# Spacing out the row scatters of a routed group in a fused attention and mixture-of-experts kernel

## The chip, the cores and the metric

The kernel runs on one core of one Trainium2 chip. The metric is the device time of one execution in microseconds (us). The kernel before the change takes 2172.19 us, the median of three runs between 2167.95 and 2175.05 us.

## What is computed

The input is 8 sequences of 1024 tokens, each token 256 float32 numbers. The reference first does `x = x + layernorm(attention(layernorm(x)))`, with 16 heads of 16 numbers and a causal mask, and then `x = x + layernorm(moe(layernorm(x)))`. The second part is what the change touches. A router gives each token scores for 8 experts; the two best experts are used with the softmax scores as weights:

```
scores = softmax(flat @ router_weight.T + router_bias)
topk_w, topk_idx = top_k(scores, 2)
gate = min(gu[..., :I], 7); up = clip(gu[..., I:], -7, 7)
down = ((up + 1) * gate * sigmoid(1.702 * gate)) @ down_proj + down_bias
out = (down[chosen] * topk_w).sum()
```

The reference computes all 8 experts for every token. The kernel computes only the two chosen ones: it sorts the tokens by expert in DRAM first.

## The kernel before

**Groups and units.** The tokens are 16 groups of 512 (t = 0 to 15), two for each sequence b. Attention runs sequence by sequence in units u of four heads: four units for a sequence, 32 in all. While the scores of unit u are computed once to find the row maxima (`sa`, L834), the scores of unit u-1 are computed again transposed, exponentiated and multiplied with the values (`sb` L929, `pT` L941, `av` L970). A unit is 9 steps of two **half steps** each, so a unit is 18 half steps and a sequence 72. After unit 31 one more round of 9 half steps does the values of the last unit alone.

**What is done in between.** Everything else of the attention part is written as generators that yield pieces: `piece(pe, dve, act, pool, after)` states what the next piece costs each engine, and that it is ready `after` half steps behind the piece before it. After each half step `pump` (L1253) adds a planned allowance to a credit for each engine (for GpSimd 1.91 us a half step, with a ceiling of 1.3) and emits ready pieces as long as every engine that they need has a credit of at least zero. Three lists are gone through in this order: `urgent` (masks, maxima and normalisation of the running units), the first job of `due` (layernorm and projections of the next sequence, which have to be there at given units), and all of `back`. The `back` list holds one job for each group, `finish(b, c)` (L1017), oldest first.

**A `back` job.** It projects the attention result (`yps`, L1031), takes its layernorm, adds x and stores the sum (`x1d`, L1052). Then it waits until the job two groups before it is done (L1053), and goes on to `route(t)` (L1074): the second layernorm (`xn`), its transposes (`x2ps`, L1092), the router logits (`lps`), softmax, ranks, the count of tokens for each expert (`cps`, L1153), the slots in DRAM (L1181), two extra columns of `xn` (L1186 and L1190), and then the eight **scatters** (L1191 to L1200): indirect DMAs issued by GpSimd, each of which writes 128 rows of `xn` to the slots of one of the two choices. The projection of a group (L1022) also waits until the job two groups before it has its `xn`. The job is done when its last scatter is issued. Jobs 11 and 15 go on to `table` (L301), which works out which expert each tile of 256 sorted rows belongs to.

**The hand-over.** When unit 31 has been emitted and the table of the first 12 groups isn't known yet, the oldest `back` jobs are emitted on the spot, with no allowance asked (L1383 to L1385), until it is; then the first sorted rows are loaded (`load_early`). The expert part then runs tile by tile. The first 14 tiles pump the rest of the `back` jobs, 12 times a tile, and before tile 14 `finish_all` (L1270) emits whatever is left.

**Order on the queues.** TensorE, VectorE, ScalarE and the SP queue run in the order of the source. On GpSimd `in_order` keeps the order of the source too, except that neighbouring scatters may change places. GpSimd also runs the causal masks (L950, L883), the reciprocal roots (L517) and most of the layernorm scaling (L529, L1050), and in the expert part one multiplication for each quarter tile (L1477).

Of the kernel before, what the change touches and what calls it, by code (L numbers as in the profile page):

```python
# [24 lines left out]
def piece(pe=0.0, dve=0.0, act=0.0, pool=0.0, after=0):  # L25


    return (pe, dve, act, pool), after
# [30 lines left out]
def attn_moe_kernel(  # L59
# [31 lines left out]
    NT = B * S // TB  # L91
# [147 lines left out]
    def in_order(put, scatter=False):  # L239

        if free[0]:
            return
        for before_it in fixed if scatter else fixed + loose:
            tc.add_manual_dep(
                put.ins, before_it,
                mybir.DependencyInfo(mybir.DependencyClass.NoSync, mybir.DependencyReason.DATA),
                reason="order of the source",
            )
        if scatter:
            loose.append(put.ins.name)  # L250
        else:
            fixed[:], loose[:] = [put.ins.name], []

    def apart(put, group):

        tc.declare_no_dep(put.ins, group=group, reason="scatters to different rows")
        tc.add_to_no_dep_group(group, put.ins)
# [284 lines left out]
    with ExitStack() as attn:  # L542
# [229 lines left out]
        n = QC // P  # L772
# [244 lines left out]
        def finish(b, c):  # L1017
# [35 lines left out]
            while nth > 1 and not finishes[nth - 2].done:  # L1053
                yield piece(after=1)
            yield from route(nth, y, last)

        def normed(dst, src):
# [16 lines left out]
        def route(t, x1, last):  # L1074
# [90 lines left out]
            for n in range(NTB):  # L1165
                nc.vector.tensor_tensor(slot[:, n, :], slot[:, n, :], so_far, ALU.add)
                after = counts[:, nth + 1, :]
                if n + 1 < NTB:
                    after = small.tile([P, E], F32, tag="after", name="after")
# [18 lines left out]
            first_of = ap2.tile([P, NTB, E], F32, tag="rank", name=f"first_{t}")  # L1188
            nc.vector.tensor_tensor(first_of, is_r[:, 0], region, ALU.mult)
            nc.vector.tensor_reduce(xn[:, :, D + 1], first_of, AX.X, ALU.add)  # L1190
            for r in range(TOPK):  # L1191
                for n in range(NTB):
                    yield piece(pool=1.1, after=0 if last and (n or r) else 1)
                    put = nc.gpsimd.indirect_dma_start(  # L1194
                        out=xs_dram[:, :],
                        out_offset=bass.IndirectOffsetOnAxis(ap=slots[:, t, r, n : n + 1], axis=0),
                        in_=xn[:, n, :], in_offset=None,
                    )
                    in_order(put, scatter=True)
                    apart(put, "xs")  # L1200
# [561 lines left out]
```

## Time and profile before

| what | before |
|---|---|
| median of the timed runs | 2172.19 us |
| the profiled execution, and its span | 2175.62 us, 2173.9 us |
| mean granted TensorE clock | 0.981 |
| TensorE busy | 2064.7 us (95%) |
| VectorE busy | 1712.1 us (79%) |
| ScalarE busy | 1061.4 us (49%) |
| GpSimd busy | 1059.4 us (49%) |
| unit 0 starts; unit 31 starts; round 32 starts; first expert tile | 24.3, 1313.1, 1355.4, 1386.8 us |
| scatters (L1194) | 128, median 976 ns each |

A table of where the groups stand was read from the timelines of VectorE and GpSimd. The half steps were counted on VectorE, which takes the maxima of each half step with its own instructions (L844, L850, L859, L865); h is the running number, 18 for each unit. "Ready" is the last column of `xn` (L1190); `x1d` is the store of the group two later, behind which that group's `route` may begin once this group's job is done.

| group | ready, us (h) | first scatter, us | last scatter, us | `x1d` of the group two later, us |
|---|---|---|---|---|
| 2 | 579.0 (249) | 579.4 | 606.5 | 630 |
| 3 | 639.7 (276) | 641.4 | 656.9 | 677 |
| 4 | 762.2 (330) | 764.6 | 780.3 | 801 |
| 5 | 823.7 (355) | 824.2 | 846.7 | 873 |
| 6 | 937.2 (402) | 939.6 | 955.4 | 975 |
| 7 | 997.6 (427) | 998.1 | 1020.2 | 1046 |
| 8 | 1110.8 (474) | 1113.1 | 1128.9 | 1150 |
| 9 | 1172.6 (499) | 1173.1 | 1195.4 | 1217 |
| 10 | 1276.3 (541) | 1276.8 | 1294.2 | 1300 |
| 11 | 1315.5 (558) | 1316.0 | 1332.7 | 1371 |

How to read it: the profile's busy shares are means over a long kernel. Attention (24 to 1387 us) and the expert part have different limits, so times are read from windows that cover one sequence (four units) each, where the work is the same from one to the next.

### The profile page before, as it was taken

What the parts mean: (1) busy time and instruction counts of PE and PEld (TensorE: products, weight loads), DVE (VectorE), ACT (ScalarE), POOL (GpSimd) and SP (SyncE); (2) the same over time, 40 slices, a digit from 0 to 9 for tenths busy, and PEclk for the clock granted to TensorE, in tenths of its full rate; (3) what the DMA queues carried; (4) which work ended last, traced back from release to release, by engine and by line L of the source; (5) the groups of instructions that cost most, each with busy time, mean ns of one, the idle gap of its engine ahead of it and who ended that gap; (6) DMA issues with size and microseconds to landing.
All of it is one profiled execution on the core that took longest, in us unless ns stands there. A gap on an engine that the chain in (4) does not pass through costs nothing.

```text
span 2173.9 us, 44649 instructions
## 1 busy us (share of the span) xinstructions
PE 2064.7 (95%) x16205; PEld 1265.7 (58%) x16205; DVE 1712.1 (79%) x4090; ACT 1061.4 (49%) x2068; POOL 1059.4 (49%) x1217
## 2 busy tenths in 40 slices
PE   7999999999999999999999998999999999999995
PEld 3444444444444434444534443678888888888884
DVE  4786887986887887887878788678767888877776
ACT  3566665666666655655655665433123232222222
POOL 3321653472474456355554645565544444544443
PEclk9899999999999999999999999999999999999998
DMA  4102102112112111112111111646867777766774
GB/s 123 19 17 46 31 29 64 34 45 45 43 35 65 26 38 46 48 46 49 48 36 41 43 38 36 222 161 213 266 247 257 269 264 264 266 240 239 270 269 152
DMA packets 147097, 254.85 MB, mean 117 GB/s; under 512 B 21505, under 2 KB 106009, under 8 KB 144953
## 3 DMA queue, kind: packets, MB, share of 16 engines
q1 hardware_dynamic: 133128, 217.01, 32.2%
q0 software_dynamic: 12528, 34.36, 4.2%
q8 instruction: 129, 2.11, 0.4%
q14 instruction: 96, 0.78, 0.1%
q10 hardware_dynamic: 1216, 0.58, 0.1%
HBM read 171.13 MB, written 55.63 MB: 104 GB/s over the span
## 4 chain that ended last, share of the span: by engine, by line
PE 69%; DVE 18%; POOL 6%; issue 3%; ACT 1%; DMA 1%; DVEq 0%; ACTq 0%; POOLq 0%; SPq 0%
PE sa L834 18%; PE gu L1461 14%; PE av L970 10%; PE dn L1501 7%; PE sb L929 6%; PE pjk L740 3%; PE yps L1031 3%; PE pjq L740 3%; PE vps L726 3%; DVE mx L850 2%; DVE sa L844 2%; DVE acc L1576 1%; POOL ytd L1514 1%; DVE gate L1470 1%; POOL xsd L1194 1%
## 5 line engine op out<-in xcount | busy, mean ns | idle before, releaser
L941 ACT ACTIVATE pT<-sb 128x512 f32<-128x512 f32 x1134 | 616.7, 595 | 394.9 <-PE sb L929 363.5
L929 PE MATMUL sb<-qP,kP 32*128 32x512 f32 (+3 forms) x3072 | 706.1, 528 | 13.4 <-ACT pT L941 11.1
L834 PE MATMUL sa<-kP,qP 32*128 32x512 f32 (+3 forms) x3072 | 656.9, 528 | 24.7 <-DVE mx L844 12.6
L1461 PE MATMUL gu<-xsT,wg 128*128 128x256 f32 (+1 forms) x2208 | 489.4, 374 | 3.1 <-ACT xsT L1441 1.9
L1461 PEld LDWEIGHTS gu<-xsT,wg 128*128 128x128 f32 x2208 | 410.0, 191 | 59.0 <-ACT xsT L1441 3.1
L850 DVE TENSOR_REDUCE mx<-sa 128x2 f32<-128x1024 f32 x256 | 310.7, 1215 | 118.1 <-PE sb L929 90.4
L950 POOL TENSOR_SCALAR_AFFINE_SELECT pT<-pT 128x512 f32<-128x512 f32 x256 | 164.5, 659 | 467.4 <-ACT pT L941 456.1
L834 PEld LDWEIGHTS sa<-kP,qP 32*128 32x128 f32 x3072 | 227.5, 185 | 248.2 <-issue 102.7
L1472 ACT ACTIVATE sig<-gate 128x256 f32<-128x256 f32 (+1 forms) x276 | 112.8, 409 | 530.6 <-DVE gate L1470 498.6
L970 PE MATMUL av<-pT,vpad 128*32 128x256 f32 (+1 forms) x5120 | 350.8, 371 | 5.0 <-DVE avs L981 3.0
L929 PEld LDWEIGHTS sb<-qP,kP 32*128 32x128 f32 x3072 | 295.4, 186 | 46.3 <-ACT pT L941 21.1
L1477 POOL TENSOR_TENSOR sig<-sig,gate 128x256 f32<-128x256 f32 (+1 forms) x276 | 199.5, 725 | 244.1 <-ACT sig L1472 240.9
L970 PEld LDWEIGHTS av<-pT,vpad 128*32 128x32 f32 x5120 | 117.3, 109 | 294.4 <-issue 237.1
L1501 PE MATMUL dn<-wd,act 128*128 128x256 f32 x1064 | 259.6, 383 | 17.5 <-DVE act L1482 15.7
L1501 PEld LDWEIGHTS dn<-wd,act 128*128 128x128 f32 x1064 | 194.2, 190 | 50.8 <-DVE act L1482 26.7
L1470 DVE TENSOR_SCALAR gate<-gu,bs 128x256 f32<-128x256 f32 (+1 forms) x276 | 128.9, 467 | 115.2 <-PE gu L1461 96.5
L844 DVE CUSTOM_DVE_ANT_0 sa<-sa,cmask 128x512 f32<-128x512 f32 x256 | 177.6, 698 | 39.8 <-PE sb L929 20.9
L1514 POOL DMA_INDIRECT ytd<-ys,places x133 | 133.8, 1006 | 128.5 <-DVE ys L1509 93.8
L1194 POOL DMA_INDIRECT xsd<-xn,slots x128 | 128.9, 1007 | 65.0 <-DVE xn L1190 35.5
L1482 DVE SCALAR_TENSOR_TENSOR act<-up,sig 128x256 f32<-128x256 f32 (+1 forms) x276 | 123.3, 447 | 25.8 <-POOL sig L1477 25.6
L869 ACT COPY edge<-sa 128x512 f32<-128x512 f32 x192 | 112.9, 588 | 40.9 <-DVE mx L859 20.1
L888 DVE TENSOR_REDUCE mx<-edge 128x8 f32<-128x1024 f32 x96 | 115.7, 1205 | 18.2 <-POOL edge L883 18.2
(243 smaller groups left out, 2343.8 us busy)
## 6 DMA issues: line engine op xcount, KB each, us to landing
wg<-_L_ffn_gate_up_proj_dram SPq DMA_DIRECT2D x69, 1024.0 KB
wd<-in_L_ffn_down_proj_dram SPq DMA_DIRECT2D x69, 512.0 KB
xs<-xsd SPq DMA_DIRECT2D x60, 258.0 KB
yy<-ytd SPq DMA_DIRECT2D x15, 1024.0 KB
bs<-biasd SPq DMA_DIRECT2D x69, 132.0 KB
x<-in_L_attn_x_dram SPq DMA_DIRECT2D x16, 512.0 KB
aT<-avn SPq DMA_DIRECT2D x256, 32.0 KB
x1d<-y SPq DMA_DIRECT2D x16, 512.0 KB
```

The lines of the kernel that those rows point to most:

```text
L834: nc.tensor.matmul(ps[:, hh, ds(at, w)], lhsT=qP[r, ts(i, P)], rhs=kP[r, ds(c * QC, w)], start=True, stop=True,)
L844: nc.vector.tensor_tensor_reduce(out=ps[:, hh, :], in0=ps[:, hh, :], in1=cmask, scale=1.0, scalar=NEG, op0=ALU.add, op1=ALU.max, accum_out ...
L850: nc.vector.tensor_reduce(mx[:, heads, i, 2:3], ps, AX.X, ALU.max)
L929: nc.tensor.matmul(banks[hh][:, ds(at, QC - off)], lhsT=kP[r, ts(j, P)], rhs=qP[r, ds(c * QC + off, QC - off)], start=True, stop=True,)
L941: nc.scalar.activation(pT[:, 2 * pair + hh, :], banks[hh], AF.Exp)
L950: in_order(nc.gpsimd.affine_select(out=d, in_=d, compare_op=ALU.is_ge, fill=0.0, base=0, pattern=[[0, HG], [1, P]], channel_multiplier=-1,))
L970: nc.tensor.matmul(av[ds(hh * HS, HS), ds(off + a - at, z - a)], lhsT=vp[:, j, ds((g * HG + hh) * VS, HS)], rhs=pT[:, hh, a:z],  start=c n ...
L1194: put = nc.gpsimd.indirect_dma_start(out=xs_dram[:, :], out_offset=bass.IndirectOffsetOnAxis(ap=slots[:, t, r, n : n + 1], axis=0), in_=xn ...
L1461: nc.tensor.matmul(ps[:, half, :w], lhsT=wg[:, kt, ds(half * FF + f * P, P)], rhs=xT[:, kt, :], start=(kt == 0), stop=(kt == KT - 1),)
L1477: in_order(nc.gpsimd.tensor_tensor(sg, sg, gt, ALU.mult))
L1501: nc.tensor.matmul(pss[n][:, 0, :], lhsT=act[:, f, ts(n, P)], rhs=wd[:, f, :], start=(f == 0), stop=(f == FT - 1),)
L1514: put = nc.gpsimd.indirect_dma_start(out=yt_dram[:, :], out_offset=bass.IndirectOffsetOnAxis(ap=places[:, i, n : n + 1], axis=0), in_=y[:, ...
```

## The change

In `route`, the pieces of the eight scatters of a group get other distances. Before, each was ready one half step behind the piece ahead of it (in the two groups of the last sequence, the seven later ones at once). After, the first is ready two half steps behind the slots in all groups, and each later one four half steps behind the one before; in the last two groups they are ready at once, as before. The condition `t == NT - 2` decides nothing, since `last` is true for group 14 as well as 15. No instruction is added or removed.

```diff
+            rest = 0 if last else 1 if t == NT - 2 else 4
             for r in range(TOPK):
                 for n in range(NTB):
-                    yield piece(pool=1.1, after=0 if last and (n or r) else 1)
+                    yield piece(pool=1.1, after=rest if n or r else 2)
                     put = nc.gpsimd.indirect_dma_start(
```

## The prediction

> **What bounds the kernel now.** I first cut attention into windows of one sequence each (four units, 72 half steps), because the work in them repeats. These are the sequences b = 2 to 7.
>
> ```profile
> core 0: us, PE busy (x) PEld busy (x) DVE busy (x) ACT busy (x) POOL busy (x), PEclk, DMA share, GB/s
> 336.30:500.60 164.30, 160.80 (x1538) 75.57 (x1534) 135.54 (x310) 102.36 (x191) 90.94 (x98) 1.00 0.19 47
> 500.60:665.30 164.70, 161.68 (x1578) 76.74 (x1574) 137.49 (x316) 104.70 (x196) 85.02 (x93) 1.00 0.18 44
> 665.30:840.40 175.10, 167.73 (x1582) 78.13 (x1578) 139.59 (x324) 105.24 (x197) 76.56 (x84) 0.97 0.17 43
> 840.40:1014.00 173.60, 166.44 (x1586) 78.51 (x1582) 140.73 (x326) 104.49 (x197) 91.17 (x98) 0.98 0.17 45
> 1014.00:1189.20 175.20, 167.18 (x1582) 78.34 (x1578) 140.88 (x325) 104.51 (x197) 91.45 (x98) 0.97 0.17 44
> 1189.20:1355.40 166.20, 152.03 (x1558) 70.53 (x1555) 140.88 (x331) 99.92 (x189) 91.03 (x102) 0.99 0.15 39
> ```
>
> The second column is the length. TensorE is busy for 98% of the first two windows, so it is the bound; VectorE has 83%. TensorE's instruction counts in the next three windows are the same within 1%, yet they take 10.4, 8.9 and 10.5 us longer than the 164.7 before, 29.8 us in all, and their clock column falls below 1.00. By units, all of it lies in the third and fourth unit of a sequence (47.4 and 44.9 us in the first case, where the sequence before has 41.7 and 40.2). So I opened the timelines of one such place, 998 to 1009 us, on GpSimd, VectorE, ScalarE and TensorE:
>
> ```profile
> 998.06 1.10 POOL L1194 DMA_INDIRECT xsd<-xn,slots  x1 [4.75 <-DVE xn L1190]
> 999.46 0.96 POOL L1194 DMA_INDIRECT xsd<-xn,slots  x1 [0.30 <-issue]
> 1000.73 0.96 POOL L1194 DMA_INDIRECT xsd<-xn,slots  x1 [0.30 <-issue]
> 1001.99 0.96 POOL L1194 DMA_INDIRECT xsd<-xn,slots  x1 [0.30 <-issue]
> ...
> 1004.01 1.23 DVE L850 TENSOR_REDUCE mx<-sa 128x2 f32<-128x1024 f32 x1 [4.04 <-PE sa L834]
> ...
> 1004.12 1.09 ACT L941 ACTIVATE pT<-sb 128x512 f32<-128x512 f32 x2 [5.02 <-PE sa L834]
> ...
> 1004.76 1.61 PE L929 MATMUL sb<-qP,kP 32*128 32x512 f32 x4 [1.77 <-ACT pT L941]
> ...
> 1007.36 1.22 PE L834 MATMUL sa<-kP,qP 32*128 32x512 f32 x2
> ```
>
> While GpSimd issues four scatters back to back, VectorE and ScalarE stand still for 4 to 5 us, both waiting for scores whose matmuls the timeline ends at 1000.0; then TensorE stands for 1.8 us because ScalarE has freed no bank; and a little later `sa` takes 1.22 us where it takes 0.70 at full clock. The trace grants half clock for 3.4 us from 1007.2.
>
> I then went through all 576 half steps for the time by which VectorE's maximum starts later than both its scores and its own last instruction allow. More than 1 us is found eight times: 1.5 and 1.5 (group 0), 1.6 (group 4), 4.4 (5), 1.6 (6), 4.0 (7), 2.3 (8) and 4.3 us (9). Each lies inside a run of four or five scatters 1.27 us apart. Of the groups 1, 2, 3, 10 and 11, which go out in ones, twos and threes but for one run of four (group 2), none shows it. The half clock follows all six of groups 4 to 9, for 6.8, 3.4, 3.4, 3.4, 6.8 and 3.4 us, so half of 27.2 us is lost, 13.6. With the six late starts (18.2 us) that is 31.8 us, close to the 29.8 from the windows. I take 29.8, and 3.0 more for group 0.
>
> A rule speaks against this reading. The Trainium skill, SBUF — State Buffer, section "SBUF: two separate sides", has only VectorE and GpSimd contend, and TensorE and ScalarE wait on no one for their SBUF ports; by it a run of scatters could not hold up scores and exponentials, the stalls would have another cause, and the gain would be nothing. The trace shows the standstill and the scatters together in seven groups of seven, so I go by the rows. TensorE: Matmul & The Clock Gate, section "Why this matters for your kernels", asks for idle gaps over some 3 us before the clock drops; the gaps here are 1.8 to 2.1 us and it drops six times, so the rows decide again (by the rule 18.2 us would be the price, not 31.8).
>
> **The change, part by part.**
>
> *Distance 4.* Number and cost of the 128 scatters stay (976 ns each). A half step is 164.7 / 72 = 2.29 us, so the scatters of a group in attention become ready 9.2 us apart and cannot queue up four at a time unless GpSimd has nothing else for some 12 half steps; the masks come in the first ten half steps of each unit, so three in a row is what can still happen (half steps 11, 15 and 19). Group 3 has such a run at 650 us, without a late maximum. I let a fifth of the 32.8 us stay: gain 26. The ends are 0 and 33.
>
> *First scatter at 2.* GpSimd waits 35.5 us in 8 places for the last column of `xn` with a scatter at the head of its queue. Queued behind it are masks, roots and scaling. TensorE waits only 13.6 us in all for masks (`av` on `pT`), 20 times, so the gain is between 0 and 13.6 and a loss at most one half step per group, which is hidden while the group isn't due. I take 0.
>
> *Lateness, in attention.* The last scatter of a group comes 2 + 28 = 30 half steps behind "ready", where the least before was 8: 22 half steps or 50 us later. Three things wait for it: `route` of the group two later, the table at group 11, and the first loads. Before, `x1d` comes 20 to 26 us behind the last scatter two groups earlier (780.3 to 801, 846.7 to 873 and so on), so the wait now takes hold: group 6 ends at 402 + 30 = 432 and not 410, and group 8 may begin there and not at 417. What it then needs is VectorE time, which is scarce in the first ten half steps of a unit, and TensorE credit, which the next sequence's projections take first. Going through the pieces, group 8 is ready at about 475 (before 474), since it then waits for fewer others. An odd group is hit harder: group 7's last scatter is near 457 to 475, so the second layernorm of group 9 comes after 458, its count of tokens (`cps`) just misses the projections that begin at half step 496, and it is ready near 517 (before 499). That repeats and does not grow. Group 11 then starts `route` at 548, and 25 to 30 half steps later, at 573 to 578, it is ready. Unit 31 ends at 576.
>
> *The hand-over.* So eight scatters and the whole table of group 11 are emitted on the spot. Before, half of the table was already:
>
> ```profile
> 1355.42 0.82 PE L417 MATMUL tabps<-two,ones 128*128 128x144 f32 x2 [3.06 <-DVE two L414]
> 1357.50 0.57 PE L438 MATMUL takenps<-each,ones 128*128 128x8 f32 x2 [1.26 <-DVE each L435]
> ```
>
> These 4.3 us become the whole chain. VectorE's table instructions from L310 to L356 take 2.3 us, and the copy of `seg` with its round trip about 0.7: 3.0 us more, and some 2 us if the slots aren't ready (`cps` to `slots` took 2.9 us for group 12). The eight scatters then are the longest run of all, in front of the masks of round 32: one stall of the above size, 5 us (29.8 / 6). Less what overlaps: 8 us in all. If the group is ready ten half steps sooner it is 3; if its logits aren't done it is 20 or more. On the SP queue the first four sorted loads stand behind the last scatter, and behind them the transfers of the last unit (issued 1366.7 us before) and the first weights (1375.6): the run would end near 1363, so nothing there is late.
>
> *Expert part.* Group 12 now does its whole route here, 7.9 us of planned VectorE cost more (the pieces from L1105 to L1190), at 1.4 a quarter tile (175.1 us from 1386.8 to 1561.9 for 14 tiles are 12.5 us a tile, 3.1 a quarter): 18 us. Much of this is hidden: its gate for group 14 moves from 1403 to about 1445, against `x1d` of 14 at 1443. Distance 4 is 4 pumps of 1.04 us here. Before, the last table pieces come at 1565 us, at the very end of the 14 pumped tiles, so there is no slack: I put 4 us on forced pieces and filled gaps. The ends are -3 (scatters of groups 12 and 13 no longer hold up L1477; 1.2 to 2.0 us gaps on `dn`) and 15.
>
> Sum: -26 + 8 + 4 = -14, to about 2161.5 for the profiled execution of 2175.62; its distance to the median (3.4) goes along: **2158**.
>
> **The rivals.**
>
> 1. *The jobs fall behind more than that.* If job 9 and 11 lose another 20 half steps, group 11 has no logits at unit 31's end, and the chain from layernorm to table is emitted with nothing between: stats, root, four scalings of 1.23 us, transposes, logits, about 20 us, ranks and slots 10, table 7, the run of scatters 5, and as much as 15 at `finish_all`: -26 + 57 = +31; with half of that +10. 2175 to 2203, slower. It decides from about 10 half steps later than I reckon. For: the limits are tight. Against: groups 12 and 13 have no projections beside them. Chance 0.18.
> 2. *The stalls stay*, since not the run of scatters but the transfers that lie beside it make them (at 1000 us SP is sending the queries and keys of the next unit). Then only the cost is left: +5 to +15, 2177 to 2187. For: group 2's run of four, with no other transfers, has no stall. Against: the units with single scatters and the same transfers have none either. Chance 0.14.
> 3. *All of it comes back and the hand-over is free*: -33 + 3 = -30, to 2142; 2138 to 2148. Chance 0.15.
>
> My own case, 2149 to 2167, has 0.53.
>
> **How the numbers follow.** The measurement tells about 0.3% (6.5 us) from no change. Faster: all of case 3, and nearly all of mine (0.50): 0.65. Same, 2165.7 to 2178.7: 0.03 of mine, 0.04 of each of the first two rivals, 0.11. Slower: 0.24. The range runs from 2138 to 2187: it leaves out the upper half of rival 1 (0.09) and a little on each side.
>
> **What the profile after would show.** Right: the windows of b = 4 to 6 at 164 to 168 us with clock 0.99 to 1.00, no run of four scatters before unit 31, no late maximum over 1 us, and before the first table matmul of the hand-over a gap of 5 to 9 us. Wrong: half clock still at the third and fourth units; the scatters of group 11 long before or its `lps` behind the end of unit 31; a first expert tile that starts later than 1375 (now 1386.8, less 26, plus 8 is 1369); more than 3 us of new gaps before tile 14.

## The result, and the profile after

| | before | after |
|---|---|---|
| median of the timed runs | 2172.19 us (2167.95 to 2175.05) | 2195.02 us (2192.36 to 2197.99) |
| profiled execution, its span | 2175.62, 2173.9 us | 2197.53, 2195.8 us |
| unit 31 starts | 1313.1 us | 1275.3 us |
| last scores (`sa`) end; round 32 starts; the hole between them | 1351.2; 1358.0; 6.8 us | 1312.6; 1356.8; 44.2 us |
| first expert tile; tile 14 | 1386.8; 1563.6 us | 1388.1; 1584.7 us |
| group 8, 9, 10, 11 ready at half step | 474, 499, 541, 558 | 517, 546, end of unit 31, end of unit 31 |

The ratio is 1.0112, with an interval of 1.0095 to 1.0129: **slower by 1.1%**, where 2158 us had been forecast. The changed source has one line more, so lines behind L1190 carry numbers higher by one: scatters L1195, `gu` L1462. In the table, round 32 starts with its first `sb` behind the last `sa`; read so, the kernel before starts it at 1358.0 (the 1355.4 given earlier is the first table matmul in front of it).

The windows of the changed kernel, sequences b = 2 to 7, cut at its own unit starts; second column the length, and near the end the granted clock:

```profile
core 0: us, PE busy (x) PEld busy (x) DVE busy (x) ACT busy (x) POOL busy (x), PEclk, DMA share, GB/s
334.80:496.10 161.30, 158.53 (x1533) 74.34 (x1529) 136.16 (x310) 101.81 (x190) 88.12 (x96) 1.00 0.19 48
496.10:660.60 164.50, 160.70 (x1582) 76.29 (x1578) 135.92 (x307) 105.16 (x197) 73.06 (x81) 1.00 0.16 38
660.60:824.90 164.30, 159.57 (x1582) 75.91 (x1578) 139.27 (x307) 104.85 (x197) 90.11 (x97) 1.00 0.18 42
824.90:995.20 170.30, 166.53 (x1577) 77.68 (x1573) 135.56 (x291) 104.70 (x196) 78.84 (x86) 0.97 0.18 43
995.20:1157.90 162.70, 157.01 (x1542) 72.90 (x1538) 138.03 (x307) 102.16 (x192) 76.84 (x84) 1.00 0.19 44
1157.90:1356.80 198.90, 157.48 (x1571) 74.65 (x1567) 153.83 (x397) 101.03 (x190) 99.76 (x111) 0.90 0.15 40
```

The three windows that took 175.1, 173.6 and 175.2 us take 164.3, 170.3 and 162.7: the stalls are gone but for one place, at 855 us, where the scatters of groups 4 and 5 happen to meet and five of them run in a row (the clock falls once more, for 3.4 us from 896.5). In the last of the three TensorE has 1542 instructions where it had 1582, so a little of that gain is work put off. The last row is the other side: 198.9 us for what took 168.8 before, at a clock of 0.90. VectorE has 397 instructions in it (331 before): work was put off to here.

TensorE's timeline where the last scores end (the bracket is its idle time before the line, and what ended it):

```profile
1313.90 0.39 PE L1153 MATMUL cps<-chosen,ones 128*128 128x32 f32 x2
1331.98 0.47 PE L1092 MATMUL x2ps<-ident,xn 128*128 128x128 f32 x1 [17.69 <-POOL xn L529]
...
1343.61 0.61 PE L1153 MATMUL cps<-chosen,before 128*128 128x32 f32 x2 [4.50 <-DVE chosen L1149]
...
1350.03 0.98 PE L363 MATMUL segps<-ident,new 128*128 128x1 f32 x4 [5.38 <-DVE new L356]
...
1354.27 0.82 PE L417 MATMUL tabps<-two,ones 128*128 128x144 f32 x2 [1.99 <-DVE mine L398]
...
1356.84 2.09 PE L929 MATMUL sb<-qP,kP 32*128 32x512 f32 x8
```

`cps` at 1313.9 is group 10's count, `x2ps` at 1332.0 the transposes of group 11: its second layernorm had not been done when the attention was over. GpSimd, with one line of VectorE, shows where part of the 17.7 us went:

```profile
1319.69 0.95 POOL L1195 DMA_INDIRECT xsd<-xn,slots  x1 [15.24 <-DVE xn L1190]
...
1321.58 0.30 DVE L512 TENSOR_SCALAR ve<-mv 128x4 f32<-128x4 f32 x1
...
1328.55 0.96 POOL L1195 DMA_INDIRECT xsd<-xn,slots  x1 [0.31 <-issue]
1329.53 1.06 POOL L517 TENSOR_TENSOR rstd<-ve,nhalf_seg 128x4 f32<-128x4 f32 x1
1330.70 4.84 POOL L529 TENSOR_SCALAR xn<-y,mv,rstd 128x256 f32<-128x256 f32 x4
```

All eight scatters of group 10, emitted on the spot, stand in GpSimd's queue in front of the root and the scaling of group 11. They take 9.8 us (1319.7 to 1329.5). The root's input `ve` (L512) is there at 1321.9, so for 7.7 of them the chain that sets the end waits for the issuing of another group's scatters.

The other loss lies ahead of tile 14. First the hand-over, then the tiles 0 to 13, in the changed kernel and (second fence) in the one before:

```profile
1314.30:1356.80 42.50, 8.77 (x41) 5.83 (x41) 17.84 (x91) 1.67 (x4) 19.86 (x20) 0.52 0.12 42
1388.10:1584.70 196.60, 175.24 (x873) 148.52 (x874) 147.70 (x456) 55.45 (x112) 123.81 (x135) 0.94 0.63 209
```

```profile
1351.20:1358.00 6.80, 2.48 (x16) 1.47 (x16) 4.74 (x21) 1.08 (x2) 2.78 (x3) 0.81 0.01 1
1386.80:1563.60 176.80, 167.00 (x835) 142.30 (x836) 139.44 (x419) 51.82 (x106) 107.65 (x120) 0.98 0.67 222
```

TensorE works for 8.8 of 42.5 us, at half clock. **The account**, from the profiled executions: attention up to the last scores 38.6 us shorter (1351.2 to 1312.6), the hole in front of round 32 37.4 longer, round 32 to the first expert tile 2.5 longer (28.8 to 31.3), tiles 0 to 13 19.8 longer (one of them, in front of tile 14, takes 26.8 us in place of 12.6), the rest 0.8 longer: +21.9, as the spans.

### The profile page after: what moved, and what is told of

It reads as the page before. It is cut to its first block, busy times and chain, and to the rows that moved or that the text cites. A ratio compares the mean times of both kernels' runs of the same rounds, so it can differ in the third digit from the quotient of the medians.

```text
span 2195.8 us, 44670 instructions
## 1 busy us (share of the span) xinstructions
PE 2054.9 (94%) x16205; PEld 1265.2 (58%) x16205; DVE 1717.4 (78%) x4090; ACT 1065.5 (49%) x2070; POOL 1061.5 (48%) x1217
## 5 line engine op out<-in xcount | busy, mean ns | idle before, releaser
L929 PE MATMUL sb<-qP,kP 32*128 32x512 f32 (+3 forms) x3072 | 693.9, 524 | 0.6 <-issue 0.6
L834 PE MATMUL sa<-kP,qP 32*128 32x512 f32 (+3 forms) x3072 | 651.3, 524 | 26.6 <-DVE mx L850 10.4
L1462 PE MATMUL gu<-xsT,wg 128*128 128x256 f32 (+1 forms) x2208 | 490.4, 375 | 3.6 <-DMA wg<-_L_ffn_gate_up_proj_dram 2.1
L1462 PEld LDWEIGHTS gu<-xsT,wg 128*128 128x128 f32 x2208 | 410.4, 192 | 59.6 <-issue 2.9
L950 POOL TENSOR_SCALAR_AFFINE_SELECT pT<-pT 128x512 f32<-128x512 f32 x256 | 164.3, 657 | 520.3 <-ACT pT L941 512.6
L929 PEld LDWEIGHTS sb<-qP,kP 32*128 32x128 f32 x3072 | 292.8, 185 | 26.8 <-ACT pT L941 5.4
L1195 POOL DMA_INDIRECT xsd<-xn,slots x128 | 130.4, 1019 | 64.7 <-issue 41.5
L1475 DVE TENSOR_SCALAR up<-gu,bs 128x256 f32<-128x256 f32 (+1 forms) x276 | 128.0, 464 | 0.0
```

The costliest lines, as they stand in the source:

```text
L834: nc.tensor.matmul(ps[:, hh, ds(at, w)], lhsT=qP[r, ts(i, P)], rhs=kP[r, ds(c * QC, w)], start=True, stop=True,)
L929: nc.tensor.matmul(banks[hh][:, ds(at, QC - off)], lhsT=kP[r, ts(j, P)], rhs=qP[r, ds(c * QC + off, QC - off)], start=True, stop=True,)
L950: in_order(nc.gpsimd.affine_select(out=d, in_=d, compare_op=ALU.is_ge, fill=0.0, base=0, pattern=[[0, HG], [1, P]], channel_multiplier=-1,))
L1462: nc.tensor.matmul(ps[:, half, :w], lhsT=wg[:, kt, ds(half * FF + f * P, P)], rhs=xT[:, kt, :], start=(kt == 0), stop=(kt == KT - 1),)
```

## The experiments

Two theories. **L**: the scatters' distance delays the end of each job, the delay grows from group to group, and what is then not done at the end of unit 31 and ahead of tile 14 is emitted with nothing beside it. **S**: runs of four or more scatters stall the scores, and spreading takes the stalls away (the prediction's reason for a gain). The texts on record use these letters or say which is meant. The experiments went out in four lots, each lot on one chip, beside runs of the kernel before on the same chip. That turned out to matter: the kernel before took 2138.6, 2165.3, 2138.7 and 2167.5 us on the four. Each lot was one chip at one time, so "chip" below stands for chip or occasion; the runs don't tell the two apart.

All runs, from their profiles: the three windows b = 4 to 6 together, the hole in front of round 32, and the expert part from its first tile to the end.

| run | us, median | before, same chip | ratio (interval) | b = 4 to 6 | hole | expert part |
|---|---|---|---|---|---|---|
| before (recorded) | 2172.2 | | | 523.9 | 6.8 | 787.1 |
| after (recorded) | 2195.0 | 2172.2 | 1.0112 (1.0095 to 1.0129) | 497.3 | 44.2 | 807.7 |
| e1 held 20 | 2168.8 | 2138.6 | 1.0141 (1.0124 to 1.0158) | 486.7 | 21.6 | 812.4 |
| e2 filled | 2177.7 | 2138.6 | 1.0177 (1.0153 to 1.0201) | 496.2 | 6.8 | 800.2 |
| e3 every 2 | 2150.0 | 2138.6 | 1.0054 (1.0037 to 1.0071) | 491.7 | 9.2 | 796.3 |
| e4 spread to 8 | 2192.0 | 2138.6 | 1.0250 (1.0233 to 1.0267) | 490.9 | 47.5 | 805.0 |
| e5 before again | 2163.7 | 2165.3 | 0.9993 (0.9972 to 1.0013) | 516.7 | 6.5 | 788.5 |
| e6 after again | 2195.8 | 2165.3 | 1.0143 (1.0115 to 1.0171) | 493.3 | 44.4 | 808.4 |
| e7 all at once | 2198.0 | 2165.3 | 1.0153 (1.0124 to 1.0182) | 524.3 | 6.7 | 792.2 |
| e8 first at 2 | 2179.3 | 2165.3 | 1.0064 (1.0040 to 1.0087) | 517.6 | 6.8 | 796.6 |
| e9 every 2 again | 2154.2 | 2138.7 | 1.0065 (1.0040 to 1.0090) | 491.7 | 9.3 | 798.7 |
| e10 two to 12 | 2142.8 | 2138.7 | 1.0025 (1.0010 to 1.0040) | 490.6 | 7.5 | 793.1 |
| e11 late two | 2136.0 | 2138.7 | 0.9988 (0.9978 to 0.9998) | 492.2 | 6.8 | 787.9 |
| e12 three to 12 | 2152.8 | 2138.7 | 1.0069 (1.0050 to 1.0088) | 484.2 | 16.0 | 803.8 |
| e13 two to 12 again | 2150.1 | 2167.5 | 0.9926 (0.9903 to 0.9950) | 494.5 | 7.2 | 788.2 |
| e14 late two again | 2166.9 | 2167.5 | 1.0004 (0.9980 to 1.0027) | 514.6 | 6.5 | 787.1 |
| e15 two, then four | 2141.6 | 2167.5 | 0.9894 (0.9855 to 0.9932) | 494.9 | 7.1 | 785.2 |

### Lateness alone: e1 and e4

e1 keeps the scatters of the kernel before and only holds the end of each job back:

```diff
                     apart(put, "xs")
+            if not last:
+                yield piece(after=20)
```

> The scatters of a group go out as before the change (one each half step), but the job counts as done only 20 half steps behind its last scatter, except in the last two groups; nothing is left out. Theory L (lateness: the change loses its time because a job that ends later holds back the job two groups later, until the hand-over after unit 31 finds groups 10 and 11 unfinished): the runs of four scatters and their stalls stay in the third and fourth units, and the hand-over and the emission before tile 14 cost what they cost in the changed kernel, some 37 and 20 us: about 2215 to 2235 us. Rival P (work put off: attention became shorter in the changed kernel only because work was moved out of it, the runs of scatters cost nothing, and the lateness only moves that work): attention gets shorter here too, by some 40 us before unit 31 ends, and the whole comes to about the changed kernel's 2195. Rival S (the spacing itself costs the time, on GpSimd and in the expert part): near 2172.

e4 spreads by four in groups 0 to 7 only:

```diff
+            rest = 0 if last else 4 if t < 8 else 1
...
-                    yield piece(pool=1.1, after=0 if last and (n or r) else 1)
+                    yield piece(pool=1.1, after=rest if n or r else 2)
```

> Distance four only for groups 0 to 7, distance one for groups 8 to 13, first scatter at two in all. Theory L: the stalls of groups 4 to 7 go (20 us), those of 8 and 9 stay; groups 8 to 11 catch up, so that group 11 has its slots at about half step 565 of 576 and the hand-over costs at most 5 us more than before, and nothing is left before tile 14: 2150 to 2162 us. Rival P: attention loses what was put off, near 2172. Rival S: no loss in the expert part, half of that in attention: 2172 to 2185.

Both lose what the changed kernel loses. In e1 the scatters are as they were and only the jobs end later: a hole of 21.6 us and 24 more in the expert part (812.4, where the kernel before has 787 to 789). In e4 the groups 8 to 11 go out at distance 1, as before, and still the hole is 47.5 us: their lag is inherited from groups 0 to 7. The groups 4, 6 and 8 of e4 are ready at 348, 438 and 517 half steps, as in the changed kernel (348, 438, 517). So lateness alone makes the loss, as theory L says; its amounts were off. For e1 it had set 43 to 63 us over the kernel before (2215 to 2235, where 2172 had been measured); it is 30.2, since the hole grew by 15 us and not by 37. For e4 it had expected groups 8 to 11 to catch up (2150 to 2162); they did not, and it took 2192.0. One thing did not fit theory S: e1 has its runs of five scatters at 363, 771, 971 and 1014 us, and no stall in any of them.

### Other spacings on the same chip: e2 and e3

e2 puts a small GpSimd operation between the scatters of groups 0 to 13; e3 is the changed kernel with distance 2.

```diff
+                    if not last and (r, n) != (TOPK - 1, NTB - 1):
+                        idle = small.tile([P, E], F32, tag="tail", name=f"idle_{t}_{r}_{n}")
+                        in_order(nc.gpsimd.tensor_tensor(idle[:, :NTB], nhalf, nhalf, ALU.pow))
```

> Scatters ready as before the change, but GpSimd does a reciprocal root of 128x4 (about 1.04 us, its result unused) behind each scatter of groups 0 to 13, so that no two scatters follow each other within 1.3 us; a job ends as early as before. Theory L says that the runs are what stalls the engines and that the rest of the change's loss is lateness: the windows of sequences 4 to 6 fall from 175 to about 165 us each, the clock there goes to 0.99 or 1.00, hand-over as before: 2142 to 2155 us, some more if GpSimd's masks get late behind the extra 8 us a group. Rival P: no gain in these windows, 2172 to 2180. Rival S: as P.

```diff
+            rest = 0 if last else 2
...
+                    yield piece(pool=1.1, after=rest if n or r else 2)
```

> The change with a distance of two half steps in place of four (first scatter two half steps behind the slots, last two groups as changed). The job ends 16 half steps behind the slots, where before it was 8 and changed 30. Theory L: group 6 ends at half step 418, one behind where the job of group 8 began before, so nearly nothing is held back; group 11 has its slots at about 560 and some scatters and the table left at 576: hand-over up to 5 us more than before; runs of four are rare, so most of the 30 us of stalls go: 2145 to 2160 us. Rival P: half way between before and changed, 2175 to 2190. Rival S: about a third of the change's loss, 2178 to 2185.

e2 is inconclusive: the kernel before has no stalls on this chip (2138.6), so there was nothing to take away, and the extra GpSimd work cost 39 us by itself. e3 has no run of more than three behind group 2 (groups 0 and 2 still have one of five, at 360 us, and one of four, at 605), and groups 4 to 11 are ready at exactly the half steps of the kernel before (330, 355, 402, 427, 474, 499, 541, 558). With the last scatter 2 + 14 = 16 half steps behind the slots no group is late (the hole is 2.4 us longer); with 30 groups 4 to 11 all are. Most of its 11 us over the kernel before lies in the expert part (796.3). That its time falls inside the 2145 to 2160 of theory L was luck, since the gain that L had counted on, the stalls, wasn't there to be had.

### The same two kernels on another chip, and the parts of the change: e5 to e8

e5 and e6 are the kernel before and the changed kernel, unedited. e7 lets all later scatters become ready at once; e8 changes only the first one's distance.

> The kernel before, unchanged, with a profile of its own. In the first experiments it took 2138.6 us, 33.6 us less than the 2172.2 recorded first. Theory S (runs of four or five scatters make the stalls in the third and fourth units of b = 4 to 6) needs the stalls wherever the runs of scatters are: windows near 175, 174 and 175 us again, about 2170, unless the end of the attention part is that much better, which nothing in this kernel would do. Theory T (the stalls are an interplay of queues that may or may not come up with the same instructions) expects windows of 162 to 166 us with the same runs of scatters in them, half clock in none of the six places, and 2136 to 2141. If the 33 us lie elsewhere (hand-over or expert part), neither theory stands and the attribution in the prediction fails for another reason.

> The changed kernel, unchanged, beside the kernel before on the same chip. Theory L (the later scatters put groups 10 and 11 behind the end of unit 31, and the hand-over and the work before tile 14 are emitted with nothing beside them) does not depend on the stalls: 2190 to 2198, since the cost is in the order of the source. Against 2138.6 the ratio would be near 1.026 in place of 1.011. If the time of the changed kernel falls by some 30 us too, the difference between the two sets of runs is the chip's and not that of the stalls, and the ratio stays near 1.011.

```diff
-                    yield piece(pool=1.1, after=0 if last and (n or r) else 1)
+                    yield piece(pool=1.1, after=0 if n or r else 1)
```

> The kernel before, with the seven later scatters of every group ready at once, as in the last two groups: eight in a row wherever GpSimd is free. Theory S expects the longest runs and so the longest stalls, twelve groups with one of about 5 us or more, +20 to +50 us on the kernel before, with half clock behind each. Theory L expects the jobs to finish up to 7 half steps sooner, no loss at the hand-over and a gain of 0 to 6 us. If runs of scatters cost nothing and nothing waits for the job's end, the time is the same within 0.3%.

```diff
+            rest = 0 if last else 1
...
-                    yield piece(pool=1.1, after=0 if last and (n or r) else 1)
+                    yield piece(pool=1.1, after=rest if n or r else 2)
```

> The kernel before, with only the first scatter of each group ready two half steps behind its slots in place of one; the later ones keep their distance of one (in groups 14 and 15 none). Theory L: a job ends one half step later, which the next group's gate can hide or turn into a missed place beside the projections: 0 to +8 us. The prediction put this part of the change at 0. Theory S has no view on it.

Here the stalls are back: e5 has windows of 171.7, 171.3 and 173.7 us, with late starts of VectorE's maxima of up to 4.2 us in the runs of scatters. e6 on the same chip has 493.3 us in the three, 23.4 less, and repeats the hole of 44.4 us: the gain and the loss of the change are both real, and the loss is the larger. e7 has the longest runs, up to eight scatters, and pays 33 us, inside what S expected (20 to 50), though not all in the stalled windows: the two profiles differ by 24.3 us, 8.9 ahead of b = 4, 7.6 in b = 4 to 6 and 8 behind; theory L's gain of 0 to 6 did not come, since its groups are ready at the half steps of the kernel before all the same: a job that ends sooner is worth nothing if it was not awaited. e8 costs 14 us, above its bounds of 0 to 8: its runs are six long, and the expert part takes 8 us more. Every group is ready when it was, so this is not lateness. Tiles 6 and 9 take 17.6 and 16.6 us, in e5 12.6 and 11.7; why was not found, and e11, with the same first distance, does not have them.

### Chip or scatters: e8 against e11

Lot three: e9 repeats e3; e10 and e12 leave the first scatter at 1 and spread groups 0 to 11 by 2 and by 3; e11 spreads by four in groups 12 and 13 only.

```diff
+            rest = 0 if last else 2 if t < NT - 4 else 1
...
+                    yield piece(pool=1.1, after=rest if n or r else 1)
```

(e10; e12 has 3 in place of the 2.)

```diff
+            rest = 0 if last else 4 if t >= NT - 4 else 1
...
+                    yield piece(pool=1.1, after=rest if n or r else 2)
```

> The kernel of e3 again (distance 2 in place of 4), to see it on another chip if this job gets one. Theory C (the runs of scatters stall TensorE's signals on some chips and not on others; the chip of the first four experiments was one without) says: no run of more than three, so no stalls, and the same 2148 to 2152 as before on every chip, with groups 4 to 11 ready at the half steps of the kernel before (330, 355, 402, 427, 474, 499, 541, 558). The ratio then depends on the kernel before alone: about 1.005 if that takes 2139, about 0.993 if it takes 2165 to 2172. Against theory C: the ratio stays at 1.005 beside a kernel before of 2165, that is, this kernel takes 2176 there.

> The first scatter one half step behind the slots as in the kernel before, the later ones of groups 0 to 11 at distance 2, those of groups 12 and 13 at distance 1. In e3 the expert part took 796 us against 788 in the kernel before, with more gaps ahead of the transposes of x2ps; if that comes from the later scatters in the pumped tiles, this kernel gives back 4 to 10 us and takes 2138 to 2147, faster than the kernel before wherever that has its stalls (0.983 to 0.992 of 2165 to 2172). If the 8 us come from the earlier start of the expert part instead, it takes 2147 to 2152 like e3.

> Distance 4 for groups 12 and 13 alone; the others as before but for the first scatter at 2. Theory L (the expert part loses because group 12 has its whole route still to do when it begins, not because of the distance inside it) expects the hand-over as in the kernel before (first expert tile some 73 to 75 us behind the start of unit 31) and an expert part of 790 to 800 us: +8 to +16 on the kernel before, much as e8. If the distance of groups 12 and 13 is what costs, the expert part takes 805 to 810 as in the changed kernel: +25 or more, with a gap ahead of tile 14.

> As e10, with distance 3 for groups 0 to 11: the last scatter comes 22 half steps behind the slots, between 15 (e10) and 30 (the changed kernel). Theory L says there is a threshold: up to it the groups are ready at the half steps of the kernel before and the hand-over costs nothing, beyond it the lag grows with each pair of groups. At 16 (e3) nothing moved, at 28 (e1) group 11 missed the end of unit 31. If 22 still fits, group 11 is ready by half step 576 and the time is within 8 us of e10; if not, the first expert tile comes 85 to 115 us behind the start of unit 31 in place of 74 to 77, and the time is 2160 to 2195. I take the second for the likelier, since group 8's gate had 15 half steps of slack at most (it begins at 417 where group 6 ended at 410 in the kernel before).

Up to group 11, e8 and e11 are the same program. Their windows b = 4 to 6, e8 first:

```profile
669.40:842.70 173.30, 168.35 (x1582) 79.29 (x1578) 136.74 (x317) 104.47 (x197) 75.42 (x83) 0.97 0.16 39
842.70:1015.00 172.30, 167.05 (x1582) 78.86 (x1578) 139.37 (x325) 104.33 (x197) 90.96 (x98) 0.98 0.17 45
1015.00:1187.00 172.00, 166.63 (x1582) 79.20 (x1579) 139.80 (x325) 104.38 (x197) 91.03 (x99) 0.98 0.17 45
```

```profile
663.90:827.90 164.00, 160.44 (x1582) 76.70 (x1578) 137.78 (x317) 104.66 (x197) 76.03 (x83) 1.00 0.17 42
827.90:992.10 164.20, 160.66 (x1582) 76.71 (x1578) 140.23 (x325) 104.54 (x197) 91.89 (x99) 1.00 0.18 47
992.10:1156.10 164.00, 160.45 (x1582) 76.71 (x1578) 140.34 (x325) 104.66 (x197) 91.90 (x99) 1.00 0.18 47
```

The same instructions, one chip slower by 8 to 9 us in each sequence. Here is one run of six scatters of group 6 in both, all engines; e8:

```profile
953.74 0.96 POOL L1195 DMA_INDIRECT xsd<-xn,slots  x1 [0.30 <-issue]
...
954.84 0.59 PE L834 MATMUL sa<-kP,qP 32*128 32x512 f32 x2
...
955.00 0.96 POOL L1195 DMA_INDIRECT xsd<-xn,slots  x1 [0.30 <-issue]
...
957.00 1.23 DVE L850 TENSOR_REDUCE mx<-sa 128x2 f32<-128x1024 f32 x1 [1.60 <-remote]
...
958.49 1.08 ACT L941 ACTIVATE pT<-sb 128x512 f32<-128x512 f32 x2 [3.95 <-PE sb L929]
...
959.14 1.12 PE L929 MATMUL sb<-qP,kP 32*128 32x512 f32 x2 [2.06 <-ACT pT L941]
```

and e11:

```profile
938.92 0.96 POOL L1195 DMA_INDIRECT xsd<-xn,slots  x1 [0.30 <-issue]
...
940.01 0.59 PE L834 MATMUL sa<-kP,qP 32*128 32x512 f32 x2
...
940.18 0.96 POOL L1195 DMA_INDIRECT xsd<-xn,slots  x1 [0.30 <-issue]
...
940.65 1.23 DVE L850 TENSOR_REDUCE mx<-sa 128x2 f32<-128x1024 f32 x1
940.75 1.08 ACT L941 ACTIVATE pT<-sb 128x512 f32<-128x512 f32 x2 [1.04 <-PE sb L929]
```

From the scores (`sa`, second pair) to their maximum it is 0.64 us in e11 (940.01 to 940.65) and 2.16 us in e8 (954.84 to 957.00), with `sb` and ScalarE's exponential 0.73 and 3.64 us (940.02 and 954.85 to 940.75 and 958.49). The scatters run at the same pace, 1.27 us apart, and in the 16 us around them 288 scatter packets and 160 others move in both, taking as long as on the other chip (medians of 166 and 17 ns). So neither the issuing of the scatters nor their transfers are slower; what comes late is the news that the scores are there. The Trainium skill, Perfetto Trace Analysis, section "Tensor Engine Instruction (MATMUL, LD_WEIGHTS)", says that the end of a matmul is an estimate and that the spreading of its semaphore is not in the profile; so a matmul's own line can't tell a late matmul from a late signal. The updates of TensorE's semaphore, which the trace also holds, can. In the run of e11 shown above each comes within 0.1 us of the modelled end. In the kernel before, at the stall of 998 to 1004 us, none comes between 998.03 and 1003.99, and then five come within 0.24 us, for work whose modelled ends lie from 1000.00 to 1002.99. The fourth, for eight matmuls (`vps`) that take 1.99 us, is 0.09 us behind the third, so these matmuls were done before and their report was held back. The runs of groups 5 and 9 show the same (830.45 to 830.68 and 1179.25 to 1179.48 us). What holds it stays open. The executions of the experiments were all recorded by the profiler (each has a span and a clock), so a part of the recording in it isn't excluded.

The other three: e9 takes 2154.2, 2 us above its expectation of 2148 to 2152, and without stalls, as expected, which decides nothing, since on this chip e11 has runs of six without stalls; e10 takes 2142.8, inside its 2138 to 2147. e11 does better than expected (788 us in the expert part, and 2136.0 where 8 to 16 us over the kernel before had been expected): the distance inside groups 12 and 13 costs nothing. So the 20 us that the changed kernel loses there go with group 12, of which nothing had been routed when the expert part began (its `x2ps` comes 20 us behind the first tile, in the kernel before 44 us ahead of it); e1, with that lateness alone, loses 24.

e12 lands between. Its group 11 has its ranks at half step 574, and only its count, slots, scatters and table are emitted on the spot; TensorE there:

```profile
1302.06 0.39 PE L1153 MATMUL cps<-chosen,ones 128*128 128x32 f32 x2
1309.81 0.99 PE L363 MATMUL segps<-ident,new 128*128 128x1 f32 x4 [7.37 <-DVE new L356]
...
1316.69 2.09 PE L929 MATMUL sb<-qP,kP 32*128 32x512 f32 x8
```

The hole is 16.0 us, 9.2 more than before. That is close to the state which the prediction had reckoned for the changed kernel (group 11 ready at 573 to 578), and to the price which it put on it (8 us). The expected time for this case (2160 to 2195) was too high; the direction, lag beyond the threshold, was right. The threshold lies between 16 half steps (e3, e9) and 22 (e12).

### Lot four, a chip with stalls again: e13 to e15

e15 is e13 with distance 4 in groups 12 and 13:

```diff
+            rest = 0 if last else 2 if t < NT - 4 else 4
```

> The kernel of e10 again. Theory C (both are needed: a chip on which the signals come late, and a run of four or more scatters) expects 2138 to 2150 on any chip, so 0.985 to 0.992 of a kernel before of 2165 to 2172, and 1.000 to 1.004 of one of 2139. Theory D (the chip alone: on a chip with stalls they come wherever transfers are under way) expects stalls here too where the chip has them, 2160 to 2172, a ratio near 1.00.

> The kernel of e11 again, with runs of six scatters in groups 4, 6 and 8. Theory C: on a chip with stalls the windows of b = 4 to 6 take about 173, 172 and 172 us as in e8, and the time is 2165 to 2180; on one without, 2136 as in e11. Theory D gives the same time as e13 within 8 us on either kind of chip.

> As e13, but groups 12 and 13 at distance 4 in place of 1. In e11 the expert part took 788 us with that distance, in e10 793 with 1. Theory L (group 12's route is all done in the pumped tiles either way once the hand-over is in time) expects 0 to -6 us against e13, 2134 to 2143. If the distance costs by itself, +4 to +15.

The kernel of e14 took 2136.0 us on the chip before and takes 2166.9 here, with windows of 171.3, 171.7 and 171.6; that of e13 and e10 stays at 2150.1 and 2142.8. (The expectation for e13 was 2138 to 2150.) They differ by 17 us, where theory D, the chip alone, allows 8. So both are needed: a chip on which the news comes late, and scatters in a row. There is no threshold at four: in the first run of groups 5, 7 and 9 the maximum starts 0.95 to 1.1 us late with two in a row (e13, e15), 1.7 to 2.9 with three (e8, e14) and 3.3 to 4.4 with four (the kernel before, e5). The windows of e15:

```profile
664.10:828.60 164.50, 161.42 (x1582) 76.72 (x1578) 139.30 (x326) 104.59 (x197) 91.56 (x99) 1.00 0.19 47
828.60:993.80 165.20, 161.43 (x1582) 76.47 (x1578) 139.28 (x325) 104.44 (x197) 91.74 (x99) 1.00 0.18 47
993.80:1159.00 165.20, 161.58 (x1586) 76.73 (x1582) 139.51 (x325) 104.56 (x197) 91.84 (x99) 1.00 0.19 47
```

Nine maxima start 0.95 to 1.5 us late in e15 even so (two in group 0's run of five, three in runs of three, four in the runs of two of groups 3, 5, 7 and 9), but the clock holds and little is lost. **e15 is faster than the kernel before on this chip**: 2141.6 us, a ratio of 0.9894 (the changed kernel took 2195.0 and 2195.8 elsewhere and wasn't run here). On a chip without stalls e15 wasn't run; its near kin e10 is slower there by 0.25% (0.10 to 0.40%).

## Why the prediction was wrong, point by point

- **The stalls: right in size and in place, incomplete in cause.** The windows b = 4 to 6 give 26.6 us (523.9 to 497.3); the term, which held group 0's stall too, said 26. On one chip e5 and e6 give 23.4, and e7, with longer runs, has 13 late starts of over 1 us where e5 has 8. What the prediction could not see is that the chip decides as well (e8 against e11), and that runs of three are not free on such a chip (e14). It set the rule of separate SBUF ports aside because scatters and standstill lay together seven times of seven; e11's runs of six without a stall show that a scatter does not hold up TensorE or ScalarE by itself, so the rule is not refuted, and what is late is the report of matmuls that were done.
- **First scatter at 2, reckoned at 0: open.** 14 us in e8, none in e14 (1.0004).
- **The step that failed is the lateness in attention**: "Going through the pieces, group 8 is ready at about 475 (before 474)" and "That repeats and does not grow." It was ready at 517, and the lag grew: group 4 is late by 18 half steps (348 for 330), group 6 by 36 (438 for 402), group 8 by 43 (517 for 474), group 9 by 47 (546 for 499). The odd groups had been looked at as the ones hit; the even ones were hit first. Group 4's softmax (L1123) comes at half step 321, where the kernel before has 318, and its choices (L1149) at 324 in both; but in the kernel before the count `cps` goes out right behind them, and in the changed one the transposes and projections of the next sequence (743.8 to 768.6 us) and the output projection `yps` of a later group (to 778.7) are there first, and `cps` follows at 784.2, half step 342. The lines of VectorE and TensorE, before and (second fence) after:

```profile
750.60 0.17 DVE L1149 TENSOR_SCALAR chosen<-rank 128x32 f32<-128x32 f32 x1
750.92 0.38 PE L1153 MATMUL cps<-chosen,before 128*128 128x32 f32 x2 [1.11 <-DVE chosen L1149]
```

```profile
745.00 0.17 DVE L1149 TENSOR_SCALAR chosen<-rank 128x32 f32<-128x32 f32 x1
...
745.99 0.66 PE L574 MATMUL xps<-ident,xn 128*128 128x128 f32 x4
...
747.79 1.98 PE L740 MATMUL pjq<-xnT,wqT 128*128 128x512 f32 x4
...
771.65 1.99 PE L1031 MATMUL yps<-woT,aT 128*128 128x256 f32 x8
...
784.23 0.41 PE L1153 MATMUL cps<-chosen,before 128*128 128x32 f32 x2
```

  Three half steps became eighteen, one whole unit. The trace shows this order; that a piece this small waits for TensorE's credit behind the large ones is read from the source. The lag of the later groups fits the same step, with each waiting for a late one; it was not followed piece by piece.
- **The hand-over, +8**: measured +37.4, and 2.5 behind it. The price was right for the state that was assumed (e12: 9.2), and the state was wrong. Rival 1 had priced the true one, a group 11 without logits: 57 us with `finish_all`, and its 2175 to 2203 holds the result. It came to 59.7 (37.4 + 2.5 + 19.8). The run of scatters, put at 5 us in front of the masks, held up group 11's own chain for 7.7. (Half of the 57 gives that rival +2.5 and not the +10 that it states; its lower bound of 2175 goes with 2.5.)
- **The expert part, +4**: measured +19.8, for the same cause; group 12 had to be done whole there. With the hand-over in time, distance 4 in groups 12 and 13 costs nothing (e11, e14, e15: 785 to 788 us, before 787 to 789).
- **Part of the gain in attention was no gain.** It came to 38.6 us, 26.6 of them in b = 4 to 6. Of the rest, 6.5 lie in units 28 to 30 (123.9 to 117.4 us), where routing had stopped being done: work put off, and paid for later without cover.
- Three of the four signs named as wrong showed: group 11's `lps` behind unit 31, the first expert tile at 1388.1 (limit 1375), new gaps of 8.3 and 3.3 us ahead of tile 14. The fourth, half clock in the third and fourth units, did not; that part of the prediction held.

## What to carry to other kernels

A delay inside a chain of jobs that wait for each other is not to be followed for one round and then called periodic: follow it until a round repeats, and look for the step that a slightly late arrival moves behind a block of other work, since there a few steps become a whole period. What fills the gaps of a bound engine is worth its full serial time once it misses the last gap; here 16 half steps of delay made no group late and 30 cost some 60 us. Where a loss is seen beside a transfer, run the same program on a second chip before it is put down to the transfer alone, and look at when the semaphore was updated, not only at when the matmul is said to end.

## What the runs showed of the hardware

- The same program took 2138.6 and 2138.7 us on two chips and 2165.3, 2167.5 and (the recorded runs) 2172.2 elsewhere; the difference lies where scatters run in a row. With no runs of four or more but for one (e10, e13) it is 2142.8 and 2150.1. Why TensorE's results are reported 1 to 4 us late there on some chips stays open: instructions, pace of the scatters, packets and their durations are alike.
- The traces tell the two kinds of chip apart by one more mark: in the nine runs on chips with stalls 119 to 168 of some 3440 updates of VectorE's semaphore are not recorded (e13 and e15 too, which have few stalls), in the eight on the others at most four.
- TensorE's clock fell to half for 3.4 to 6.8 us behind idle gaps of about 2 us (e8: gap of 2.06 us up to 959.1, half clock from 961.8), six times between 700 and 1200 us in the kernel before and never between 76 and 1321 us in e15. The Trainium skill, TensorE: Matmul & The Clock Gate, section "Why this matters for your kernels", has gaps of over some 3 us; these rows have less. In the changed kernel the clock fell at 858.9 us, beside the late reports of 855 us, with no gap over 0.61 us in the 8 us before; the gaps are counted from modelled ends, and no run here shows the true ones.
